# Layer 0 of a two-layer graph network: one ring of four PSUM banks, a group's rows transposed ahead of its sums, the bias added last

## The chip, the cores and the metric

The kernel runs on one core of one Trainium2 chip. The metric is the device time of one launch in microseconds (us); lower is better. A profiled execution gives the trace that the text reads: TensorE (PE, with its weight loads as PEld), VectorE (DVE), ScalarE (ACT), GpSimd (POOL) and the queue of SyncE (SP), each with its instructions, their times and what each waited for.

## The reference, cut to what matters

Two layers work on 32 samples of 512 rows with 256 features, with an adjacency of 512 x 512 per sample. Each has a graph part and a feed-forward part behind a layer norm. Layer 0, the one that is changed, computes:

```python
# graph convolution on the normed rows, added to the rows
h = einsum('bnf,fu->bnu', x, W_msg)
messages = einsum('bij,biu->bju', adj, h) / max(deg, 1)
out = relu(einsum('bnf,fu->bnu', x, W_upd) + messages + bias)

# feed-forward on the normed rows: 256 -> 1024 -> 256
t = max(xx[:, None, :] + Wt[None, :, :], axis=-1) + bt     # 1024 maxima over 256 sums
trop = s * cvx(t) + (1 - s) * ccv(t)                       # piecewise linear
fused = g * trop + (1 - g) * gelu(xf @ Wc + bc)            # g = sigmoid(xf @ Wg + bg)
out = fused @ Wd + bd
```

Layer 1 is an attention over the neighbours and a token mixer of slices. Nothing of its arithmetic is changed.

## The kernel before, in words

**Stages.** `layer0_sorted` runs first. While its last groups run it already draws on `layer1_plain` for that layer's weights; then layer 1 follows. Behind both stands a slower way (`layer0`, `layer1`) that is taken only if the flags in `over` say that a row needed more candidates than were provided for.

**Convolutions.** The samples are taken in four segments of eight. `conv_in` loads `x` and `adj` (SP queue), converts `adj` to floats on GpSimd, norms the rows (`layer_norm_T`: ScalarE writes `xna`, TensorE transposes it into two banks `lnpa`, ScalarE copies these to `x1T`) and forms `ph`, the product with `W_msg`. `conv_out` forms `pu`, the product with `W_upd` (VectorE reads it into `u`, L416), and `pm`, the sums over the neighbours (VectorE reads it into `deg`, L425, and `u`, L427). It writes each row with its norm's shift and scale, a count of candidates and its eight largest entries with their places. `put_in_order` then ranks a segment's 4096 rows by their number of candidates.

**Groups.** A segment in that order makes 32 tiles of 128 rows, and eight groups of four tiles. `CAPS` says how many candidates a tile needs, from 24 down to 1. For each group three functions run:

- `sums` gathers the four tiles of rows into `xs` (L541, an indirect DMA from GpSimd). For each tile in turn ScalarE norms it to `xn` (L562), TensorE transposes it into the two banks `xsp` (L565), GpSimd adds the output bias `bd` to the rows (L566), VectorE compares the count with the cap (L580), ScalarE turns the first gathered row of the table into `best` (L583), and for every further candidate a row is gathered (`rows`, L586, four buffers) and joined on VectorE (L589). When all four tiles are through, ScalarE copies the two `xsp` banks to `xnT` (L596).
- `mixed` works on eight slices of 128 hidden features: the products `clsp` and `gatep` (L609), their functions on ScalarE (L611), four transposes of `best` into `tz` (L616), the piecewise linear part `acc` on ScalarE and VectorE (L618 to L627).
- `down` forms the products `po` with `Wd` (L638, two banks for the four tiles), which VectorE adds to `xs` (L640); SP then stores the rows.

**PSUM.** The eight banks are four pairs by tag: "tp" for everything transposed on the way in (`lnpa`, `xsp`, weights), "mm" for `ph`, `pu`, `pm`, `po` and the ranking, "mf" for `clsp` and `gatep`, "tz" for `tz`. A new tile waits until one of its tag's two banks has been read.

**Order.** `woven` interleaves the sums of the next group with the slices of the present one, and that whole stream with the convolutions of later segments. A planner then orders the instructions of each engine by priority and readiness and assigns the buffers; each engine runs its list in that order.

Of the kernel before, what the change touches and what calls it, by code (L numbers as in the profile page):

```python
# [8 lines left out]
F32 = mybir.dt.float32  # L9
I32 = mybir.dt.int32  # L10
BF16 = mybir.dt.bfloat16
U32 = mybir.dt.uint32
AF = mybir.ActivationFunctionType
ALU = mybir.AluOpType
# [4 lines left out]
P = 128  # L19
N = 512  # L20
D = 256
NT = N // P
DC = D // P
# [9 lines left out]
def layer_norm_T(nc, sb, ps, ident, eps, x, xnT, name, kept=None, pool=False):  # L33


    mv = sb.tile([P, NT, 2], F32, tag="ln_mv", name=f"mv{name}", bufs=2)
    for t in range(NT):
        st = sb.tile([P, 6], F32, tag="ln_st", name=f"st{name}_{t}", bufs=4)
        nc.vector.bn_stats(st, x[:, t, :])
        nc.vector.bn_aggr(mv[:, t, :], st)  # L40
    rs = sb.tile([P, NT], F32, tag="ln_rs", name=f"rs{name}", bufs=2)
    if pool:
        deviation(nc, rs, mv[:, :, 1], eps)
        shift = sb.tile([P, NT], F32, tag="ln_shift", name=f"shift{name}", bufs=2)
        nc.vector.scalar_tensor_tensor(shift, mv[:, :, 0], -1.0, rs, ALU.mult, ALU.mult)
    else:
        nc.scalar.activation(rs, mv[:, :, 1], AF.Sqrt, bias=eps[:, 0:1])
        nc.vector.reciprocal(rs, rs)
    pt = [ps.tile([P, NT, P], F32, tag="tp", name=f"lnp{name}_{c}") for c in range(DC)]
    for t in range(NT):  # L50
        if kept is None:
            xn = sb.tile([P, D], F32, tag="ln_xn", name=f"xn{name}_{t}", bufs=3)
        else:
            xn = kept[:, t, :]
        if pool:
            nc.scalar.activation(xn, x[:, t, :], AF.Identity, bias=shift[:, t : t + 1], scale=rs[:, t : t + 1])
        else:
            nc.vector.tensor_scalar(xn, x[:, t, :], mv[:, t, 0:1], rs[:, t : t + 1], ALU.subtract, ALU.mult)
        for c in range(DC):
            nc.tensor.transpose(pt[c][:, t, :], xn[:, c * P : (c + 1) * P], ident)  # L60
    for c in range(DC):
        nc.scalar.copy(xnT[:, c, :], pt[c].rearrange("p t n -> p (t n)"))
# [34 lines left out]
def layer0_sorted(tc, ident, eps, x, adj, w, x2s, ranks, over, following):  # L97
# [6 lines left out]
    nc = tc.nc  # L104
# [22 lines left out]
    with ExitStack() as ctx:  # L127
# [27 lines left out]

        count_to = cst.tile([P, P], I32, tag="count_to", name="count_to")
# [23 lines left out]
        def bounds(raw):  # L180
# [7 lines left out]
            pt = ps.tile([P, 2, DC, P], F32, tag="tp", name="extp")  # L188
# [19 lines left out]
        def features(raw):  # L208
# [9 lines left out]
            for i, name in enumerate(("Wc", "Wg")):  # L218
                wr = rtile("wraw", [P, DC, FFN], bufs=2)
                nc.sync.dma_start(wr, w[name].rearrange("(c p) f -> p c f", p=P))  # L220
                for f0 in range(0, FC, 2):
                    pt = ps.tile([P, NT, P], F32, tag="tp", name=f"{name}p{f0}")
                    for k in range(2 * DC):
                        f = f0 + k // DC
                        nc.tensor.transpose(pt[:, k, :], wr[:, k % DC, f * P : (f + 1) * P], ident)
                    nc.scalar.copy(rows[:, f0 : f0 + 2, (2 + i) * D : (3 + i) * D],
                                   pt.rearrange("p (f c) d -> p f (c d)", f=2))
                    yield
# [126 lines left out]
            def turn(dst, src, name):  # L355
                for c in range(DC):
                    for f0 in range(0, FC, NT):
                        pt = ps.tile([P, NT, P], F32, tag="tp", name=f"{name}p{c}_{f0}")
# [17 lines left out]
        def conv_in(b):  # L376
# [13 lines left out]
            for t0 in range(0, NT, 2):  # L390
                ph = ps.tile([P, 2, D], F32, tag="mm", name=f"ph{b}_{t0}")
# [9 lines left out]
        def conv_out(b, counts):  # L401
# [5 lines left out]
            for t0 in range(0, NT, 2):  # L407
                two = slice(t0, t0 + 2)
                pu = ps.tile([P, 2, D], F32, tag="mm", name=f"pu{b}_{t0}")
# [8 lines left out]
                for k in range(2):  # L418
                    t = t0 + k
                    pm = ps.tile([P, N], F32, tag="mm", name=f"pm{b}_{t}")  # L420
# [40 lines left out]
        def put_in_order(s, counts):  # L461
# [12 lines left out]
            pc = ps.tile([P, N], F32, tag="mm", name=f"totp{s}")  # L474
# [5 lines left out]
            pr = ps.tile([P, N], F32, tag="mm", name=f"rankp{s}")  # L480
# [30 lines left out]
            po = ps.tile([P, N], F32, tag="mm", name=f"orderp{s}")  # L511
# [19 lines left out]
        def feed_forwards():  # L531


            def sums(s, g):
# [11 lines left out]
                pt = [ps.tile([P, NT, P], F32, tag="tp", name=f"xsp{s}_{g}_{c}") for c in range(DC)]  # L546
# [9 lines left out]
                ask(0)  # L556
                for t, tile_no in enumerate(tiles):
                    if t + 1 < NT - 1:
                        ask(t + 1)
# [6 lines left out]
                    nc.gpsimd.tensor_add(r[:, :D], r[:, :D], bd)  # L566
                    vals, idxs = r[:, VAL : VAL + 8], r[:, IDX : IDX + 8]
                    if cap > 8:
                        rounds = -(-cap // 8)
                        tops = sb.tile([P, 2, 8 * rounds], F32, tag=f"tops{rounds}", name=f"tops{s}_{g}_{t}", bufs=1)  # L570
                        vals, idxs = tops[:, 0, :], tops[:, 1, :]
                        for i in range(rounds):
# [3 lines left out]
                            if i + 1 < rounds:  # L576
# [3 lines left out]
                    nc.vector.tensor_scalar(over[:, s * ST + tile_no : s * ST + tile_no + 1],  # L580
                                            r[:, COUNT : COUNT + 1], 2.0 * cap + 1.0 - D, None, ALU.is_gt)
                    m = best[t]
                    nc.scalar.activation(m, m, AF.Identity, bias=vals[:, 0:1])  # L583
                    for k in range(1, cap):
# [10 lines left out]
                for c in range(DC):  # L595
                    nc.scalar.copy(xnT[:, c, :], pt[c].rearrange("p t n -> p (t n)"))  # L596
# [34 lines left out]
            def down(s, g):  # L631
                xg, acc = got.pop((s, g))
                for t0 in range(0, NT, 2):
                    po = ps.tile([P, 2, D], F32, tag="mm", name=f"po{s}_{g}_{t0}")
# [215 lines left out]
def layer1_plain(tc, ident, eps, x2s, ranks, adj, w, out, over, ps):  # L850
# [35 lines left out]
    with ExitStack() as ctx:  # L886
# [11 lines left out]
        def psum(tag, name):  # L898
            return ps.tile([P, N], F32, tag=tag, name=name)
# [75 lines left out]
        with tc.tile_pool(name="raw", bufs=2, side="right") as raw:  # L975

            def load_T(dst, src, name):

                R, Ccols = src.shape
                for r0 in range(0, R, P):  # L980
# [3 lines left out]
                    pt = psum("tp", f"{name}p{r0}").rearrange("p (c r) -> p c r", r=P)  # L984
# [16 lines left out]
            def twice_T(src, name):  # L1001
# [5 lines left out]
                pt = psum("tp", f"{name}p")  # L1007
# [50 lines left out]
        def masks(b, bank="any"):  # L1058
# [7 lines left out]
            def turn(t):  # L1066
                pt = ps.tile([P, NT, P], BF16, tag=bank, name=f"maskp{b}_{t}")
# [1156 lines left out]
```

## Time and profile before

| what | value |
|---|---|
| median of 3 runs | 4619.27 us (4611.98 to 4620.72) |
| profiled execution, time | 4623.49 us |
| profiled execution, span | 4621.6 us |
| mean granted TensorE clock | 0.951 |
| TensorE busy (matmul) | 4067.9 us, 88% of the span |
| VectorE busy | 3379.1 us, 73% |
| ScalarE busy | 2291.7 us, 50% |
| GpSimd busy | 1729.5 us, 37% |

The table is of one execution. A busy share is an average over stages with different limits, so the text goes by stages: the opening up to about 320 us (the first segment's convolutions and the preparation of the tables), the groups of layer 0 up to about 2440 us, and layer 1. The first two stages are the ones in which `layer0_sorted` runs. In a row of waits, the engine, line and tile that waited stand left of the arrow, and what ended the wait stands right of it.

### The profile page before, as it was taken

To read this page: it belongs to the slowest core of one execution; us is meant where nothing else is said; L and a number is where in the kernel's file an instruction comes from. 1 tells how busy PE (TensorE), PEld (TensorE's weight loads), DVE (VectorE), ACT (ScalarE), POOL (GpSimd) and SP (SyncE) were. 2 spreads that over 40 slices of the span, in tenths; PEclk is the share of its full clock that TensorE was granted. 3 is DMA by queue.
4 is the path that set the end of the run, shared out by engine and by line. 5 is a ranking of instruction groups with operands and counts; after the bars stand their busy time and mean duration, and the time that the engine had idled before them with its cause. 6 is when DMAs were issued, how large, how long until landed. Compare 5 with 4: busy or idle time off the path is not lost. (4 is left out here: it accounts for less than half of the span.)

```text
span 4621.6 us, 56127 instructions
## 1 busy us (share of the span) xinstructions
PE 4067.9 (88%) x19287; PEld 2525.4 (55%) x19287; DVE 3379.1 (73%) x7040; ACT 2291.7 (50%) x4756; POOL 1729.5 (37%) x2027
## 2 busy tenths in 40 slices
PE   5768898988988889888897899999999999999987
PEld 4545655656556566555554355555555555555555
DVE  6678778887788877777775777777787777777763
ACT  2344555545655556555564444545544454454432
POOL 2356444653435534353332223222323323332220
PEclk8889999999999999998998999999999999999998
DMA  5556433653436533374431111111111111111100
GB/s 125 172 158 214 164 127 126 198 178 124 136 118 198 177 129 112 99 263 145 141 115 48 53 46 56 51 48 44 44 54 49 56 56 53 47 54 56 40 14 15
DMA packets 235100, 474.09 MB, mean 103 GB/s; under 512 B 38299, under 2 KB 114075, under 8 KB 234804
## 3 DMA queue, kind: packets, MB, share of 16 engines
q0 software_dynamic: 80256, 282.38, 19.3%
q1 hardware_dynamic: 154548, 188.02, 13.3%
q8 instruction: 154, 2.52, 0.2%
q14 instruction: 142, 1.16, 0.1%
HBM read 413.16 MB, written 57.16 MB: 102 GB/s over the span
## 5 line engine op out<-in xcount | busy, mean ns | idle before, releaser
L609 PE MATMUL clsp<-xnT,wc 128*128 128x512 f32 x1024 | 512.1, 621 | 77.3 <-ACT cls L611 63.0
L609 PE MATMUL gatep<-xnT,wg 128*128 128x512 f32 x1024 | 497.7, 605 | 16.0 <-ACT gate L611 13.2
L638 PE MATMUL po<-wd,acc 128*128 128x256 f32 x2048 | 450.9, 381 | 0.4 <-DVE acc L627 0.3
L638 PEld LDWEIGHTS po<-wd,acc 128*128 128x128 f32 x2048 | 391.4, 191 | 65.9 <-issue 13.8
L422 PE MATMUL pm<-h,adj 128*128 128x257 f32 x1024 | 295.5, 435 | 136.3 <-DVE xs L640 67.3
L589 DVE SCALAR_TENSOR_TENSOR best<-rows,xs,best 128x1024 f32<-128x1024 f32 x212 | 276.1, 1305 | 165.4 <-ACT best L583 98.1
L623 DVE SCALAR_TENSOR_TENSOR acc<-past,fld,acc 128x512 f32<-128x512 f32 x448 | 351.1, 787 | 54.3 <-ACT past L622 45.5
L1198 DVE SCALAR_TENSOR_TENSOR att<-own,other,mask 128x512 f32<-128x512 f32 x512 | 378.9, 762 | 11.5 <-DMA own<-ownd 11.0
L586 POOL DMA_INDIRECT rows<-table,xs x212 | 261.1, 1232 | 237.3 <-DVE best L589 171.8
L609 PEld LDWEIGHTS gatep<-xnT,wg 128*128 128x128 f32 x1024 | 195.8, 195 | 260.5 <-issue 197.0
L622 ACT ACTIVATE past<-tz,fld 128x512 f32<-128x512 f32 x448 | 291.0, 694 | 83.4 <-DVE acc L623 83.0
L618 ACT ACTIVATE acc<-tz,fld 128x512 f32<-128x512 f32 x256 | 199.5, 779 | 265.1 <-PE tz L616 262.0
L422 PEld LDWEIGHTS pm<-h,adj 128*128 128x128 f32 x1024 | 212.4, 218 | 194.5 <-issue 106.7
L1231 PE MATMUL avp<-att,hv 128*64 128x512 f32 x1024 | 310.3, 628 | 4.2 <-DVE att L1198 4.2
L609 PEld LDWEIGHTS clsp<-xnT,wc 128*128 128x128 f32 x1024 | 185.7, 197 | 222.3 <-issue 121.1
L1331 PE MATMUL yTp<-sw,x 128*128 128x512 f32 x512 | 242.7, 614 | 39.8 <-DVE sw L1326 32.3
L611 ACT ACTIVATE cls<-clsp,fld 128x512 f32<-128x512 f32 x256 | 176.7, 690 | 201.7 <-PE clsp L609 86.9
L1319 PE MATMUL lgp<-wsl,x4T 128*128 128x512 f32 x512 | 252.0, 628 | 27.9 <-DVE mask L1070 21.7
L1139 POOL DMA_INDIRECT x<-x2s,ranks x128 | 140.9, 1101 | 343.0 <-DVE att L1198 104.1
L1284 POOL TENSOR_TENSOR mu<-mu,eps 128x16 f32<-128x16 f32 x32 | 121.3, 3791 | 324.2 <-DVE mu L1283 323.1
L611 ACT ACTIVATE gate<-gatep,fld 128x512 f32<-128x512 f32 x256 | 175.6, 686 | 127.5 <-PE gatep L609 103.6
L541 POOL DMA_INDIRECT xs<-rows_of,order x128 | 143.4, 1121 | 250.7 <-DVE acc L623 78.7
(597 smaller groups left out, 8961.5 us busy)
## 6 DMA issues: line engine op xcount, KB each, us to landing
adji<-in_adj SPq DMA_DIRECT2D x128, 256.0 KB
ai<-in_adj SPq DMA_DIRECT2D x128, 256.0 KB
own<-ownd SPq DMA_DIRECT2D x128, 256.0 KB
rows_of<-keep SPq DMA_DIRECT2D x32, 550.0 KB
x<-in_x SPq DMA_DIRECT2D x32, 512.0 KB
x2s<-xs SPq DMA_DIRECT2D x32, 512.0 KB
out<-x SPq DMA_DIRECT2D x32, 512.0 KB
rows<-table,xs POOLq DMA_INDIRECT x212
```

Source lines behind the costliest of these rows:

```text
L422: nc.tensor.matmul(pm[:, : D + 1], a[:, i, t * P : (t + 1) * P], h[:, i, :], start=i == 0, stop=i == NT - 1)
L586: nc.gpsimd.indirect_dma_start(out=row, out_offset=None, in_=table, in_offset=bass.IndirectOffsetOnAxis(ap=idxs[:, k : k + 1].bitcast(U32) ...
L589: nc.vector.scalar_tensor_tensor(m, row, vals[:, k : k + 1], m, ALU.add, ALU.max)
L609: nc.tensor.matmul(pf, wf[:, c, f * P : (f + 1) * P], xnT[:, c, :], start=c == 0, stop=c == DC - 1)
L611: nc.scalar.activation(o, pf, fn, bias=fld[:, f, bf : bf + 1], scale=1.0 if fn == AF.Gelu else 0.5)
L622: nc.scalar.activation(r, z, AF.Relu, bias=fld[:, f, AT + b : AT + b + 1])
L623: nc.vector.scalar_tensor_tensor(y, r, fld[:, f, CH + b : CH + b + 1], y, ALU.mult, ALU.add)
L638: nc.tensor.matmul(po[:, i, :], acc[f][:, t * P : (t + 1) * P], wd[:, f, :], start=f == 0, stop=f == FC - 1)
L1198: nc.vector.scalar_tensor_tensor(e, own[h], other[:, j, h : h + 1], mask[:, j, :], ALU.max, ALU.mult)
L1231: nc.tensor.matmul(pv[q][k * HO : (k + 1) * HO, :], hv[:, j, h, :HO], weighed[b, h, j], start=j == 0, stop=j == NT - 1)
L1319: nc.tensor.matmul(pf, xnT[:, c, t * P : (t + 1) * P], wsl[:, c, :], start=c == 0, stop=c == DC - 1)
L1331: nc.tensor.matmul(py, xn[:, t, c * P : (c + 1) * P], sw[:, t, :], start=t == 0, stop=t == NT - 1)
```

## The change

What it does, in four parts:

1. The tags "tp" and "mm" become one tag "mm" with four banks, for the convolutions, the transposes on the way in, the ranking, the down projection and the weights that layer 1 prepares. "mf" and "tz" stay.
2. In `sums` the first three gathers from the table are asked for at once; then all four tiles are normed and transposed and the two banks copied to `xnT`; then come the sums of the four tiles.
3. The four comparisons of a group with their caps become one, against a table `limits` that nine fills on GpSimd write at the start.
4. The four additions of `bd` stand at the end of `sums`.

The diff, cut to its core (the other tiles of tags "tp" and "mm" get `tag="mm", bufs=4` in the same way; the `psum` of `layer1_plain`'s opening too):

```diff
@@ layer_norm_T
-    pt = [ps.tile([P, NT, P], F32, tag="tp", name=f"lnp{name}_{c}") for c in range(DC)]
+    bank = {"tag": "mm", "bufs": 4} if pool else {"tag": "tp"}
+    pt = [ps.tile([P, NT, P], F32, name=f"lnp{name}_{c}", **bank) for c in range(DC)]
@@ layer0_sorted
+        limits = cst.tile([P, ST], BF16, tag="limits", name="limits")
+        for i, cap in enumerate(CAPS):
+            if i == 0 or cap != CAPS[i - 1]:
+                nc.gpsimd.memset(limits[:, i:], 2.0 * cap + 1.0 - D)
...
-                    pm = ps.tile([P, N], F32, tag="mm", name=f"pm{b}_{t}")
+                    pm = ps.tile([P, N], F32, tag="mm", name=f"pm{b}_{t}", bufs=4)
...
@@ sums
-                pt = [ps.tile([P, NT, P], F32, tag="tp", name=f"xsp{s}_{g}_{c}") for c in range(DC)]
+                pt = [ps.tile([P, NT, P], F32, tag="mm", name=f"xsp{s}_{g}_{c}", bufs=4) for c in range(DC)]
...
-                ask(0)
+                for t in range(NT - 1):
+                    ask(t)
+                tops = []
                 for t, tile_no in enumerate(tiles):
-                    if t + 1 < NT - 1:
-                        ask(t + 1)
                     r, cap = xg[:, t, :], CAPS[tile_no]
                     xn = sb.tile([P, D], F32, tag="xn", name=f"xn{s}_{g}_{t}", bufs=2)
                     nc.scalar.activation(xn, r[:, :D], AF.Identity, bias=r[:, MEAN : MEAN + 1],
                                          scale=r[:, MEAN + 1 : MEAN + 2])
                     for c in range(DC):
                         nc.tensor.transpose(pt[c][:, t, :], xn[:, c * P : (c + 1) * P], ident)
-                    nc.gpsimd.tensor_add(r[:, :D], r[:, :D], bd)
...
-                    nc.vector.tensor_scalar(over[:, s * ST + tile_no : s * ST + tile_no + 1],
-                                            r[:, COUNT : COUNT + 1], 2.0 * cap + 1.0 - D, None, ALU.is_gt)
-                    m = best[t]
+                    tops.append((vals, idxs))
+                for c in range(DC):
+                    nc.scalar.copy(xnT[:, c, :], pt[c].rearrange("p t n -> p (t n)"))
+                nc.vector.tensor_tensor(over[:, s * ST : (s + 1) * ST].rearrange("p (t g) -> p g t", g=NG)[:, g, :],
+                                        xg[:, :, COUNT], limits.rearrange("p (t g) -> p g t", g=NG)[:, g, :],
+                                        ALU.is_gt)
+                for t, tile_no in enumerate(tiles):
+                    m, (vals, idxs) = best[t], tops[t]
                     nc.scalar.activation(m, m, AF.Identity, bias=vals[:, 0:1])
-                    for k in range(1, cap):
+                    for k in range(1, CAPS[tile_no]):
...
                     if t == NT - 2:
                         ask(NT - 1)
                     yield
-                for c in range(DC):
-                    nc.scalar.copy(xnT[:, c, :], pt[c].rearrange("p t n -> p (t n)"))
+                for t in range(NT):
+                    nc.gpsimd.tensor_add(xg[:, t, :D], xg[:, t, :D], bd)
                 got[s, g] = xg, xnT, best
@@ down
-                    po = ps.tile([P, 2, D], F32, tag="mm", name=f"po{s}_{g}_{t0}")
+                    po = ps.tile([P, 2, D], F32, tag="mm", name=f"po{s}_{g}_{t0}", bufs=4)
```

## The prediction

> **What bounds the kernel now.** I read the page first, then the windows by stage, then TensorE's waits in each stage, then the order of time around one long wait. The windows' columns are start:end and length, then busy us of PE, PEld, DVE, ACT and POOL, the granted clock, the DMA share and GB/s.
>
> ```profile
> span 4621.6 us, 56127 instructions
> PE 4067.9 (88%) x19287; PEld 2525.4 (55%) x19287; DVE 3379.1 (73%) x7040; ACT 2291.7 (50%) x4756; POOL 1729.5 (37%) x2027
> ```
>
> ```profile
> 0.00:320.00 320.00, 203.04 (x853) 158.47 (x854) 205.34 (x756) 108.90 (x232) 115.73 (x312) 0.84 0.51 149
> 320.00:2440.00 2120.00, 1868.90 (x6982) 1210.48 (x6981) 1639.59 (x3067) 1172.44 (x1980) 1010.82 (x1266) 0.95 0.48 153
> 2440.00:4621.60 2181.60, 1996.01 (x11457) 1156.47 (x11454) 1534.16 (x3220) 1010.33 (x2545) 602.96 (x449) 0.97 0.15 47
> ```
>
> TensorE is the busiest engine in the two long stages; in the opening it is level with VectorE. Layer 0 is the first two rows: an opening of 320 us with 117 us of idle TensorE, and 2120 us of groups with 251 us of it (66 us per group). The third row is layer 1. Of TensorE's waits (engine, line, tile, what ended the wait: us, times, longest) these belong to the banks that the change touches, the opening first:
>
> ```profile
> PE pm L422 <- DVE u L416: 31.3, 8, 14.1
> PE pu L413 <- DVE u L427: 15.5, 5, 11.2
> PE pm L422 <- DVE u L427: 4.8, 2, 4.2
> ```
>
> ```profile
> PE pm L422 <- DVE xs L640: 67.3, 16, 8.0
> PE clsp L609 <- ACT cls L611: 62.5, 40, 6.3
> PE pm L422 <- DVE u L427: 20.2, 9, 6.2
> PE ph L395 <- DVE xs L640: 16.0, 2, 8.6
> ...
> PE pm L422 <- DVE u L416: 7.8, 6, 2.2
> ```
>
> `pm` does not read `xs` or `u`: it waits because one of the two "mm" banks is held until VectorE has read the tile in it. With a row of 1.6 us for `ph`, the opening loses 53 us to this. The group stage loses 67.3 + 20.2 + 16.0 + 7.8 = 111 us. The second row (banks "mf") is not touched. One such wait, VectorE and then TensorE:
>
> ```profile
> 999.51 3.90 DVE L589 SCALAR_TENSOR_TENSOR best<-rows,xs,best 128x1024 f32<-128x1024 f32 x3 [1.19 <-DMA rows<-table,xs]
> 1003.88 1.28 DVE L589 SCALAR_TENSOR_TENSOR best<-rows,xs,best 128x1024 f32<-128x1024 f32 x1 [0.47 <-DMA rows<-table,xs]
> 1005.09 0.68 DVE L640 TENSOR_TENSOR xs<-xs,po 128x512 f32<-128x512 f32 x1
> ```
>
> ```profile
> 1005.92 3.77 PE L422 MATMUL pm<-h,adj 128*128 128x257 f32 x8 [7.10 <-DVE xs L640]
> ```
>
> The read of `po` stands on VectorE behind sums that wait for gathered rows; `pm` needs that bank 7.10 us before it comes free.
>
> The other engines' waits that the change touches, in the group stage:
>
> ```profile
> POOL xs L566 <- ACT xn L562: 215.4, 52, 14.6
> DVE over L580 <- DMA xs<-rows_of,order: 46.1, 45, 6.7
> ACT best L583 <- DMA best<-table,xs: 121.0, 70, 5.0
> ```
>
> **What the Trainium skill says.** "Perfetto Trace Analysis", section "Matmuls": independent groups should rotate through different PSUM banks, so that an evacuation runs beside the next group's matmuls. The trace agrees: 111 us above are two groups meeting in one bank. "PSUM — Partial Sum Buffer", section "Engine vs sequencer instructions": VectorE, ScalarE and GpSimd take their queue strictly in order and matmuls run in program order. The trace agrees: GpSimd stood 215.4 us before the bias additions with gathers queued behind. "TensorE: Matmul & The Clock Gate", section "What's actually happening": an idle window of about 3.4 us halves the clock until about 3.4 us of work have passed. The trace fits: 0.91 granted in the 100 us from 1000, which hold the wait of 7.10 us, against 0.99 in the next 100.
>
> **The change, part by part.** Both programs were built, not run, so that order and bank of every tile can be listed. From its first matmul, layer 1 has the same order in both on all five engines, so the third row stays.
>
> 1. *One ring of four banks.* Work is neither added nor taken away. For each reuse of a tp or mm bank I counted TensorE's work between the last write of the old tile and the first of the new (0.86 us for a 128x512 f32 product, from the start-to-start of the cls and gate products; 0.43 for 256 columns; 0.11 for a transpose). In the opening 68 of 121 reuses have under 2 us of it before, 14 of 118 after. I keep 53 x 14/68 = 11 us, so 42 leave the TensorE row; since VectorE, level with TensorE there, and a chain of features also lead to the first group, I let half count: **21 us**. In the group stage the reuses behind a VectorE reader with under 3 us are 38 before and 28 after, under 2 us 23 and 11. Those of the conv directly behind `po`, which cost 83.3 us, are 16 under 3 us before; in their place stand 4 (two `xsp`, two `pm`). So between 111 x 10/38 = 29 and 111 x 12/23 = 58 us go by count, and 83.3 x 12/16 = 62 from `po` alone; I take 55, and let 45 count, since TensorE then arrives sooner at the cls and gate banks (62.5 us of waits): **45 us**.
> 2. *The clock behind those waits.* 18 waits behind `po` average 4.6 us. If half exceed 3.4 us, each is followed by 3.4 us at half speed, so 1.7 us lost: 9 x 1.7 = 15 us, and I take **12**. Bounds 0 and 30 (all 18).
> 3. *Rows first.* The same 128 activations, 256 transposes and 64 copies (615, 291 and 597 ns) move ahead of the sums; a group's two transpose banks are held for fewer of its steps. The three first gathers of a group stand ahead of all else that it asks of GpSimd after the rows; on SP loads of `x` and `adj` shift by a few places, with no wait added. Moved transposes wait for `xn`, which has two buffers; the transposes waited 4.0 us for it in the stage. I set 0, between -10 and +20, covered by the products of the group before.
> 4. *Bias last.* 128 additions of 925 ns stay on GpSimd; the wait of 215.4 us leaves its queue, and gathers move up. VectorE waits for gathered rows 61.9 + 28.2 = 90 us; a third of it, where VectorE is over 80% busy (9 of 21 windows of 100 us), gives 90 x 1/3 x 9/21 = 13, I take **8**. The reader of the sum is one group later, so lateness has 66 us of cover; without it four additions, 3.7 us a group, would show. SP's output transfers wait for the same reader and don't move.
> 5. *One comparison a group.* 128 x 144 ns become 32 of about 180 (the 128x4 operation at L438 took 179): 13 us off VectorE. Of 46 us of waits for rows, one in four stays: 35 off. Of these 48 us I count a quarter, for the stretches where VectorE leads: **12**. Should the single comparison wait for the last of four gathers at 1.3 us more each, 32 x 1.3 = 42 us come back.
> 6. *Nine small fills on GpSimd* at the start: 0.1 us by the row of a 128x4 fill, 0.9 at most by a 128x512 cast. 1 to 8 us, beside the first loads; 0.
>
> Sum: 21 + 45 + 12 + 0 + 8 + 12 = 98 us, from 4623.5 for the profiled execution to 4525.5. The median of the runs, 4619.3, is 4 us lower than that execution, so 4521.
>
> **Rivals.** *A, the wait moves to the next bank.* VectorE's backlog is as long as before, and TensorE meets it at `cls`, `gate` and `tz` (62.5 + 14.2 + 13.2 + 10.8 = 101 us today). For it: in the example VectorE reads `u` right behind `po`. Against: it is 77% busy in that stage. A fifth of 53 + 111 would stay: 33 us, 4586.
>
> *B, slower: ScalarE becomes the gatekeeper of the conv's banks.* In the shared ring 36 conv products per run take, with under 3 us of work in between, a bank that ScalarE frees by copying `xsp` or `lnpa`; before, none took a bank of either. ScalarE is in order and stands in front of gathered `best` tiles for 121.0 us in 70 waits of up to 5.0. If each of the 36 costs 2.7 us, the 98 are gone; at 3.4 us it is 4521 + 122 = 4643. Against: today 37 reuses between `xsp` and `lnpa` with as little work cost 2.0 + 1.1 us of TensorE.
>
> *C, it doesn't do what it says:* with two `xn` buffers and four banks the planner still puts the third and fourth rows behind the next products, as its list does in several groups, and all stays within 0.2%: 4619.
>
> *D, more:* all 164 us of bank waits go and the clock's 15 with them: about 4440.
>
> **How the numbers follow.** Forecast 60% (4521, its own range 4475 to 4580), A 18%, B 12%, C 5%, D 5%. The range from 4455 to 4625 leaves out most of D and of B, some 15%. A measurement of this kernel can tell about 0.2% (9 us) from no change: faster 0.82, nearly all of forecast, A and D; same 0.06; slower 0.12.
>
> **What would show it.** Right: `pm` behind `xs` falls from 67 to under 20 us, the opening ends by 300 us, the comparison and the bias rows lose their waits, the clock in the group stage rises to 0.96, and layer 1 stays within 5 us of 2182. Wrong: `pm` or `pu` waits for `xnT` or `x1T` in tens of us (B), or the rows of `clsp` and `gatep` grow by what `pm` lost (A). An opening that ends no earlier takes 21 us out.

## The result, and the profile after

The change made the kernel slower: 4654.27 us, median of 4 runs (4651.98 to 4656.92), against 4618.99 us before (4 runs). The ratio is 1.0079, with a 95% interval from 1.0062 to 1.0097. The prediction was 4521 us, with a range up to 4625 us.

From the page of the changed kernel (the profiled execution took 4651.98 us):

```profile
span 4650.2 us, 56060 instructions
PE 4067.5 (87%) x19287; PEld 2513.5 (54%) x19287; DVE 3396.6 (73%) x6944; ACT 2295.1 (49%) x4756; POOL 1728.7 (37%) x2036
```

The windows by stage, with the columns as before the change:

```profile
0.00:320.00 320.00, 182.58 (x819) 148.40 (x819) 193.29 (x706) 97.40 (x208) 106.37 (x299) 0.82 0.48 142
320.00:2440.00 2120.00, 1863.77 (x6931) 1200.72 (x6932) 1644.25 (x2987) 1165.89 (x1968) 1018.74 (x1287) 0.94 0.48 154
2440.00:4650.00 2210.00, 2021.14 (x11539) 1164.41 (x11537) 1559.05 (x3252) 1031.78 (x2580) 603.59 (x451) 0.97 0.15 46
```

The same work is done: TensorE is busy for the same 4067 us. In the opening it gets through 819 matmuls by 320 us where it got through 853. For the rest the trace gives better marks than fixed windows do: the first `clsp` of the first group (end of the opening) and the first transpose of layer 1 (end of the groups). By these marks the groups before ran on to 2514.6 us, so the third row of the windows, read as layer 1 until now, holds 75 us of groups as well.

| | opening ends | groups end | groups take | layer 1 takes |
|---|---|---|---|---|
| before | 324.0 | 2514.6 | 2190.6 | 2107.0 |
| after | 341.4 | 2540.9 | 2199.5 | 2109.3 |

So the opening lost 17.4 us instead of gaining 21, the groups lost 8.9 us instead of gaining 77, and layer 1 stayed. Such marks come from one execution each: bias_only (below), whose time is that of the kernel before, shows 2179.0 us of groups, so differences of some 10 us between marks decide nothing alone. TensorE's waits in the opening, then in the groups (320 to 2480 us):

```profile
PE lnpa L61 <- ACT xna L57: 84.5, 8, 21.3
PE totp L482 <- DVE mine L478: 13.0, 1, 13.0
...
PE ph L401 <- DVE u L422: 6.3, 1, 6.3
```

```profile
PE clsp L619 <- ACT cls L621: 94.8, 36, 6.5
PE xsp L571 <- ACT xn L568: 34.9, 20, 6.4
PE clsp L619 <- ACT gate L621: 26.6, 11, 5.1
PE lnpa L61 <- ACT xna L57: 24.5, 2, 17.4
PE xsp L571 <- DVE xs L650: 19.7, 7, 5.4
...
PE pm L428 <- DVE xs L650: 7.0, 2, 4.1
```

The bank waits are gone as predicted: the opening's 53 us behind `u` are down to the 6.3 us of `ph` and about 1 us of `pm`, and the groups' 67.3 us of `pm` behind `xs` to 7.0. In their place TensorE stands before the next transposes (`lnpa`, which waits for ScalarE's `xna`) and before `clsp` (62.5 us before). The row of `lnpa` in the opening before:

```profile
PE lnpa L60 <- ACT xna L56: 38.6, 9, 17.5
```

The other engines' rows in the groups after:

```profile
POOL xs L606 <- ACT xn L568: 60.5, 13, 11.1
...
DVE over L588 <- DMA xs<-rows_of,order: 91.3, 21, 5.8
...
ACT best L593 <- DMA best<-table,xs: 122.8, 78, 9.4
```

The row to look at is the second. The prediction expected the comparison's 46.1 us of waits to fall to a quarter. They doubled, in half as many waits.

What such a wait does is seen in one of the last groups, which have no convolutions beside them. VectorE, then ScalarE, then TensorE (start, duration, instruction, idle time before it and what ended it):

```profile
2334.29 1.29 DVE L637 SCALAR_TENSOR_TENSOR acc<-acc,cls 128x512 f32<-128x512 f32 x1
2340.29 0.17 DVE L588 TENSOR_TENSOR over<-xs,limits 128x4 f32<-128x4 f32 x1 [4.71 <-DMA xs<-rows_of,order]
2340.38 2.47 DVE L633 SCALAR_TENSOR_TENSOR acc<-past,fld,acc 128x512 f32<-128x512 f32 x3
```

```profile
2346.91 0.69 ACT L621 ACTIVATE cls<-clsp,fld 128x512 f32<-128x512 f32 x1 [3.22 <-DVE acc L637]
```

```profile
2339.92 1.88 PE L619 MATMUL gatep<-xnT,wg 128*128 128x512 f32 x4
...
2347.65 3.78 PE L619 MATMUL clsp<-xnT,wc 128*128 128x512 f32 x4 [4.45 <-ACT cls L621]
```

A comparison of 0.17 us, whose result nobody needs before the end of the layer, holds VectorE for 4.71 us until the last of four gathers has landed. Behind it stands `acc`; ScalarE's next `cls` needs a buffer that `acc` still holds; TensorE's next `clsp` needs the bank that this `cls` has to read. After the gap of 4.45 us the same four products take 3.78 us where those ahead of it took 1.88: the granted clock from 2347.6 to 2351.3 us is 0.50. The four gathers had been asked for late themselves. Before the first of them GpSimd stood behind VectorE:

```profile
2331.56 1.22 POOL L547 DMA_INDIRECT xs<-rows_of,order  x1 [10.11 <-DVE acc L633]
```

Groups 27 to 29 (counted from 0), which lie here, take 58.2 us each from one first `clsp` to the next, and took 52.6. The text calls these three the last groups.

### The profile page after: what moved, and what is told of

It reads as the page before. It is cut to its first block, busy times and chain, and to the rows that moved or that the text cites. A ratio compares the mean times of both kernels' runs of the same rounds, so it can differ in the third digit from the quotient of the medians.

```text
span 4650.2 us, 56060 instructions
## 1 busy us (share of the span) xinstructions
PE 4067.5 (87%) x19287; PEld 2513.5 (54%) x19287; DVE 3396.6 (73%) x6944; ACT 2295.1 (49%) x4756; POOL 1728.7 (37%) x2036
## 5 line engine op out<-in xcount | busy, mean ns | idle before, releaser
L619 PE MATMUL clsp<-xnT,wc 128*128 128x512 f32 x1024 | 545.2, 657 | 126.6 <-ACT cls L621 95.3
L619 PEld LDWEIGHTS gatep<-xnT,wg 128*128 128x128 f32 x1024 | 205.5, 203 | 278.2 <-issue 226.6
L596 POOL DMA_INDIRECT rows<-table,xs x212 | 249.3, 1176 | 194.7 <-DVE best L599 145.6
L428 PE MATMUL pm<-h,adj 128*128 128x257 f32 x1024 | 261.8, 398 | 14.8 <-DVE xs L650 7.0
L558 POOL DMA_INDIRECT best<-table,xs x128 | 146.3, 1143 | 266.8 <-PE tz L626 219.8
```

Source lines behind the costliest of these rows:

```text
L428: nc.tensor.matmul(pm[:, : D + 1], a[:, i, t * P : (t + 1) * P], h[:, i, :], start=i == 0, stop=i == NT - 1)
L596: nc.gpsimd.indirect_dma_start(out=row, out_offset=None, in_=table, in_offset=bass.IndirectOffsetOnAxis(ap=idxs[:, k : k + 1].bitcast(U32) ...
L619: nc.tensor.matmul(pf, wf[:, c, f * P : (f + 1) * P], xnT[:, c, :], start=c == 0, stop=c == DC - 1)
```

## The experiments

Ratios are to the kernel before, run beside each kernel on the same chip, with their 95% intervals; 0.0010 is 4.6 us. "Comparison" is how a group's counts are compared with the caps: four or one on VectorE, left out, or on GpSimd.

| kernel | banks | sums | comparison | median us | ratio |
|---|---|---|---|---|---|
| ring_only | ring | as before | four | 4614.83 | 0.9998 [0.9988, 1.0008] |
| no_ring | pairs | changed | one | 4624.09 | 1.0014 [1.0008, 1.0021] |
| bias_only | pairs | bias last only | four | 4613.62 | 0.9996 [0.9989, 1.0003] |
| late_turn | ring, `lnpa` late | changed | one | 4622.45 | 1.0012 [1.0000, 1.0024] |
| turn_nocmp | ring, `lnpa` late | changed | left out | 4550.53 | 0.9861 [0.9833, 0.9888] |
| turn_old_tail | ring, `lnpa` late | changed, last groups as before | one, last groups four | 4582.86 | 0.9934 [0.9910, 0.9958] |
| turn_ask | ring, `lnpa` late | changed, gathers one by one | one | 4610.78 | 0.9985 [0.9970, 1.0000] |
| ring_turn | ring, `lnpa` late | bias last only | four | 4622.22 | 1.0024 [1.0014, 1.0034] |
| after_nocmp | ring | changed | left out | 4538.08 | 0.9826 [0.9801, 0.9852] |
| before_nocmp | pairs | as before | left out | 4546.39 | 0.9857 [0.9828, 0.9887] |
| no_ring_nocmp | pairs | changed | left out | 4558.22 | 0.9871 [0.9840, 0.9902] |
| turn_gp | ring, `lnpa` late | changed | on GpSimd | 4550.02 | 0.9847 [0.9820, 0.9875] |
| after_tile | ring | changed | four | 4640.07 | 1.0055 [1.0032, 1.0077] |
| ring_nocmp | ring | as before | left out | 4522.72 | 0.9807 [0.9790, 0.9823] |
| after_gp | ring | changed | on GpSimd | 4549.73 | 0.9858 [0.9841, 0.9874] |
| open_turn_gp | ring, `lnpa` late in the opening | changed | on GpSimd | 4543.01 | 0.9843 [0.9826, 0.9859] |
| ring_gp | ring | as before | on GpSimd | 4531.19 | 0.9821 [0.9804, 0.9839] |
| ring_open_gp | ring, `lnpa` late in the opening | as before | on GpSimd | 4520.57 | 0.9798 [0.9779, 0.9816] |

**1. The parts alone.** ring_only is the kernel before with the tags changed and nothing else:

```diff
-    pm = ps.tile([P, N], F32, tag="mm", name=f"pm{b}_{t}")
+    pm = ps.tile([P, N], F32, tag="mm", name=f"pm{b}_{t}", bufs=4)
...
```

(every tile of tags "tp" and "mm" likewise)

> The kernel before with the ring of four banks alone: the sums, the comparisons and the bias additions stand as they stood before. Theory 1 (the ring ties TensorE to the order in which the program takes banks, so the next sample's transposes lnpa stand between pm of tile 0 and pm of tile 1): the first ranking product totp starts at 269 us as in the changed kernel (before: 254), and the group stage loses more than the changed kernel does, because xsp now keeps two of the ring's four banks through a whole group's sums: 4660 to 4720 us. Theory 2 (the ring itself costs nothing, the rows-first sums cost all): totp at 254 us, time 4600 to 4620 us.

`totp` is the ranking's first product; it starts at 253.6 us in the kernel before and at 269.0 in the changed one. The opening of ring_only lost what the changed kernel's lost (totp at 269.7 us), but the groups won it back: no difference, 0.9998. So both theories missed: the first in the whole, the second in the opening. no_ring is the changed kernel with the two pairs of banks back:

> The changed kernel on two pairs of banks as before (tags tp and mm), everything else as changed: rows first, three gathers asked at once, one comparison, bias last. Theory 1: totp back at 254 us (+-3) and the whole at 4615 to 4640 us, as only the rows-first part is left. Theory 2 (rows first and the three early gathers put ScalarE's xn and xnT and GpSimd's gathers ahead of the running group's work): the opening is back, but groups 25 to 31, which have no convolutions beside them, keep their loss of 26 us, and the time is above 4640 us.

The opening was back (totp at 255.6 us) and the last groups kept their loss (58.2 us each), but the whole is where theory 1 put it. Neither part alone costs much; together they cost 1.0079. bias_only moves the four additions and nothing else:

```diff
-                    nc.gpsimd.tensor_add(r[:, :D], r[:, :D], bd)
...
+                for t in range(NT):
+                    nc.gpsimd.tensor_add(xg[:, t, :D], xg[:, t, :D], bd)
```

> The kernel before with the four additions of bd moved to the end of a group's sums, nothing else. The prediction's own step gave 8 us: 4611 us, with the 215 us of GpSimd's waits for xn gone. If GpSimd's queue only hands the wait on to the next instruction of its list (a gather that waits for its bank of best, or for its candidates), the time stays within 4 us of 4619 us.

GpSimd's waits after that edit, in the groups:

```profile
POOL xs L600 <- ACT xn L564: 215.1, 48, 14.6
```

The wait is there as before (215.4 us), and by ratio the time fell by 2 us of the 8, which cannot be told from nothing. Moved in the program, the additions did not move behind their wait in the engine's list. With the ring as well it is 268.0 us (ring_turn, below); only with rows first is it short: 60.5 us in the changed kernel, 81.8 in late_turn. There GpSimd waits elsewhere: its early gathers of `best` stand 219.8 us behind `tz` in the changed kernel's groups, and stood 84.8.

**2. The order that the ring imposes.** TensorE's list for the opening runs `pu`, `pm` of tile 0, `pm` of tile 1 and so on with pairs of banks, and the next sample's `lnpa` come in between as their rows get ready. With the ring, in ring_only too, all eight `lnpa` stand behind `pm` of tile 0 and ahead of `pm` of tile 1, which is the order in which the program takes the banks. TensorE before and after the change, in the opening:

```profile
111.45 1.20 PE L422 MATMUL pm<-h,adj 128*128 128x257 f32 x2 [4.23 <-DVE u L427]
112.44 1.06 PE L60 MATMUL lnpa<-ident,xna 128*128 128x128 f32 x4
113.29 1.06 PE L422 MATMUL pm<-h,adj 128*128 128x257 f32 x2
```

```profile
92.47 1.90 PE L428 MATMUL pm<-h,adj 128*128 128x257 f32 x8
115.64 2.17 PE L61 MATMUL lnpa<-ident,xna 128*128 128x128 f32 x8 [21.27 <-ACT xna L57]
117.60 2.93 PE L428 MATMUL pm<-h,adj 128*128 128x257 f32 x8
```

After the change the next `pm` stands behind transposes whose rows are not normed yet. late_turn moves those transposes in the program:

```diff
-            layer_norm_T(nc, sa, ps, ident, eps, xg, x1T, f"a{b}", pool=True)
+            for _ in norm_in_steps(nc, sa, ps, ident, eps, xg, x1T, f"a{b}"):
+                yield
...
-                yield from woven(conv_out(b, counts[:, i * NT : (i + 1) * NT]), 8, after, 2)
+                yield from woven(conv_out(b, counts[:, i * NT : (i + 1) * NT]), 6, after, 3)
```

(`norm_in_steps` is `layer_norm_T` with a yield between the statistics and the rest; the counts by which the streams are woven rise by one step a sample)

> The changed kernel, with one thing moved in the program: the norm's ScalarE steps and the transposes lnpa of the next sample are emitted behind pm of tile 2 in place of behind pm of tile 0, so that they take their banks there; its loads and statistics stay where they are (the weaving counts are raised by one step a sample to keep the pace). Theory 1: TensorE no longer stands at lnpa before pm of tile 1, the waits of lnpa for xna in the opening fall from 84 us to under 50 us, totp comes at 250 to 259 us instead of 269 us, and the whole at 4625 to 4645 us. Theory 2: the opening's loss is the longer way from pm through deg to u, so totp stays at 265 us or later and the time within 6 us of 4654 us.

TensorE's waits in the opening, in late_turn:

```profile
PE lnpa L84 <- ACT xna L82: 48.0, 8, 20.3
...
PE pm L452 <- DVE u L446: 15.4, 1, 15.4
```

The wait of `lnpa` fell to 48.0 us, totp came at 261.5 us (half of the loss at that mark), the first `clsp` at 323.3, and the whole fell by 31 us (1.0079 to 1.0012), a little more than theory 1 had it. Taken alone it would confirm that theory. It doesn't: without the comparison the same edit is not faster (turn_nocmp 0.9861, after_nocmp 0.9826), so most of the 31 us are not the price of this order. ring_turn tests it with the sums as before:

> The ring of four banks, the late transposes lnpa of late_turn and bias last; the sums as before in all else (gathers one by one, rows tile by tile, four comparisons). If the ring's loss in the opening (17 us) and its gain in the groups (22 us, both read in the ring alone) are two separate things, this keeps the gain without the loss: 4590 to 4602 us. If the gain in the groups came only from the start that was 17 us later (convolutions and groups meeting at other times): 4612 to 4618 us.

Missed by both: 4622 us, slower than ring_only. Late `lnpa` beside the groups is no gain in itself; where it was used in the opening alone it was (6, below).

**3. What holds the last groups.** Three kernels built on late_turn. turn_nocmp takes the comparison out:

```diff
-                nc.vector.tensor_tensor(over[...], xg[:, :, COUNT], limits[...], ALU.is_gt)
+        nc.gpsimd.memset(over[:, : B * NT], 0.0)
```

> late_turn without the comparisons of the counts with the caps (they are left out; one fill of the flags stands in their place). In late_turn groups 25 to 31 take 58 us each where the kernel before takes 52 us, and in each of them VectorE stands 4.7 us at the one comparison, which waits for the last of the four gathers, with acc behind it. Theory 3 (the one comparison is what costs the last groups): 52 to 53.5 us a group and 4592 to 4602 us as a whole. Theory 2 (rows first costs them: all four xn, eight xsp and two xnT of the next group stand in the running group's lists of ScalarE and TensorE, and wait for the gathers themselves): 56 us a group or more, and within 8 us of 4622 us.

The last groups fell from 58.0 to 50.4 us each, and the whole by 72 us (4622 to 4551), far more than the last groups hold. turn_old_tail gives the last segment's groups their old sums from the third on:

> late_turn, with the sums of the last segment's groups from its third on in the order of the kernel before (gathers asked one by one, four comparisons, rows transposed tile by tile); only bias last is kept in them. Theories 2 and 3 both: the groups from 26 on go back to 52 to 53 us, and the whole to 4590 to 4604 us, faster than the kernel before. If the loss of the last groups came from the ring (po and xsp in one ring) or from the bias additions, they stay at 57 to 58 us and the whole at 4622 us.

Its last groups take 51.9 us and the whole is 4583 us, somewhat better than expected; so ring and bias additions are not what held them. turn_ask:

```diff
-                for t in range(NT - 1):
-                    ask(t)
+                ask(0)
...
+                    if t + 1 < NT - 1:
+                        ask(t + 1)
```

> late_turn with the gathers of best asked one by one again, inside the loop over the tiles as before. Theory of the early gathers (three gathers of best at the head of GpSimd's list wait for the transposes tz of the running group, 20 us each in the last groups, with the convolutions' rsb and the bias additions behind them): GpSimd's wait of best for tz falls from over 200 us to under 120 us and the time by 8 us or more, to under 4614 us. If GpSimd has time for it: within 4 us of 4622 us.

The theory missed in its mechanism: GpSimd's wait of `best` for `tz` is 195.2 us (195.7 in late_turn). The time fell by 12 us (1.0012 to 0.9985) with intervals that touch, so nothing is concluded from it.

**4. The comparison, alone.** after_nocmp takes the comparison out of the changed kernel, before_nocmp the four out of the kernel before, no_ring_nocmp and ring_nocmp out of the two kernels with one part each:

> The changed kernel without the one comparison a group (left out; a fill of the flags stands in its place), and nothing else: the transposes lnpa of the next sample still stand ahead of pm of tile 1. Theory 3 (the comparison, which waits on VectorE for the last of four gathers, is the change's main cost): the 91 us of VectorE's waits leave, the last groups take 50 to 52 us each, the whole 4575 to 4600 us. Theory 1 (the order of the ring is the main cost, and the comparison mattered only once that was mended): above 4615 us. Either way the opening stays 15 us longer (totp at 266 to 270 us).

> The kernel before without its four comparisons a group (left out in the same way). They wait 46 us in all there. If it is one comparison for four that made the wait costly (it waits for the last gather, where each of the four waited for its own), this gains little: 4600 to 4612 us. If every comparison on VectorE at that place is costly, the gain is near the whole wait or above it: under 4580 us.

> The changed kernel on two pairs of banks (as no_ring) and without the comparison. It tells what the ring is worth once neither its order nor the comparison is in the way, beside the ring with late transposes and without the comparison (4550 us). If the ring is worth the 20 us that the waits of pm for xs promised: 4565 to 4580 us. If rows first alone frees the banks in time: 4545 to 4558 us.

> The kernel before with the ring alone and without the comparisons (left out). Beside it stand without comparisons: before 4546 us, rows first on two pairs 4558 us, both together 4538 us. If ring and rows first only work together (xsp holds two of the ring's banks through a group's sums as long as the rows are not first): 4550 to 4565 us. If the ring is the part that gains and rows first only costs: 4520 to 4535 us.

after_nocmp is faster than either theory had it: 4538 us, although its opening is as long as the changed kernel's (totp at 266.4 us). TensorE's list is the same in both, instruction for instruction, and the other engines' lists differ in a few rows; so the difference is waiting, and the clock that goes with it. before_nocmp (4546 us) is far below what its first theory had: the four comparisons were costly as well. no_ring_nocmp (4558 us) fell at the upper end of its second theory, but the difference to the ring, 0.9871 to 0.9826, is the 20 us of the first all the same. ring_nocmp (4523 us) fell where its second theory put it: the ring gains, rows first costs. The groups of the changed kernel, then those of after_nocmp, each from 320 us to the end of its groups:

```profile
320.00:2540.00 2220.00, 1953.03 (x7250) 1254.78 (x7250) 1703.97 (x3079) 1215.56 (x2047) 1032.42 (x1302) 0.94 0.46 148
```

```profile
320.00:2428.00 2108.00, 1913.48 (x7250) 1240.61 (x7250) 1697.25 (x3039) 1209.49 (x2042) 1049.33 (x1295) 0.96 0.48 156
```

The same 7250 matmuls in 112 us less. TensorE is idle for 195 us instead of 267, and busy for 40 us less, at a clock of 0.96 instead of 0.94. Most of the idle time that left is this row, 94.8 us in the changed kernel:

```profile
PE clsp L613 <- ACT cls L615: 37.2, 28, 3.8
```

Rival A had expected this row to grow because the backlog moves on to the next bank. It grew, but the comparison was the reason.

Set against each other, with what the comparison cost (difference of the ratios, times 4619 us) and how long VectorE waited at it in the whole run:

| banks, sums | with | without | cost | VectorE's wait |
|---|---|---|---|---|
| pairs, as before | 1 | 0.9857 | 66 us | 58.0 us |
| ring, as before | 0.9998 | 0.9807 | 88 us | 92.1 us |
| pairs, changed | 1.0014 | 0.9871 | 66 us | 71.5 us |
| ring, changed | 1.0079 | 0.9826 | 117 us | 103.2 us |

The waits at the comparison's own line, first the kernel before, then ring_only, no_ring and the changed kernel:

```profile
  DMA xs<-rows_of,order: 58.0, 52
```

```profile
  DMA xs<-rows_of,order: 92.1, 79
```

```profile
  DMA xs<-rows_of,order: 71.5, 22
```

```profile
  DMA xs<-rows_of,order: 103.2, 23
```

Two things follow. Each microsecond that VectorE waits at the comparison costs about one of the whole: 0.9 to 1.1 in these four pairs, and 0.8 in a fifth, late_turn and turn_nocmp (70 us for 89.0 us of waits). A reservation: with the changed sums TensorE's order is the same with and without the comparison, but for one or two instructions. With the sums as before it is not, so 66 and 88 us are not the wait alone. Nor is the wait everything: ring_turn, with late `lnpa` and bias last, waits 20 us less there than ring_only (71.9 us) and takes 12 us longer.

And without the comparison the ring gains: 0.0050 (23 us) with the old sums, clear of the intervals, and 0.0045 (21 us) with the new, where they overlap. The new sums cost 0.0014 (6 us) on pairs and 0.0019 (9 us) on the ring, which is inside the intervals. With the comparison on GpSimd (6, below) their cost on the ring is clear of them: 0.0037 (17 us, after_gp against ring_gp) and 0.0045 (21 us, open_turn_gp against ring_open_gp). With the comparison on VectorE the ring's gain is eaten in ring_only and turned round in the changed kernel.

**5. One for four.** after_tile undoes part 3 of the change alone:

```diff
-                nc.vector.tensor_tensor(over[...], xg[:, :, COUNT], limits[...], ALU.is_gt)
+                    nc.vector.tensor_scalar(over[...], xg[:, t, COUNT : COUNT + 1], 2.0 * CAPS[tile_no] + 1.0 - D, None, ALU.is_gt)
```

> The changed kernel with its part 3 alone undone: four comparisons a group, one in each tile's sums, each against its own cap; ring, rows first and bias last stay. If one comparison for four is what turned the change into a loss: VectorE's waits of over for xs fall from 91 us to about 50 us, and the time by 30 to 50 us to 4605 to 4625 us. If four comparisons that stand close together behind rows first wait for the last gather just as one does: within 8 us of 4654 us.

VectorE's waits in the groups:

```profile
DVE over L585 <- DMA xs<-rows_of,order: 86.7, 74, 3.7
```

The second theory is the nearer one: 1.0055, by ratio 11 us under the changed kernel, with overlapping intervals. Four comparisons behind rows first wait nearly as long (86.7 us in 74 waits) as one does (91.3 in 21). So the exchange of one for four is a small part of the loss. What lengthened the waits stands in the other rows: from 46.1 us in the groups before to 81.0 with the ring alone, and to 59.0 with the changed sums alone.

**6. Whole kernels without that wait.** after_gp and turn_gp move the comparison to GpSimd, at the end of a group's sums; ring_gp does it with the sums as before:

```diff
-                nc.vector.tensor_tensor(over[...], xg[:, :, COUNT], limits[...], ALU.is_gt)
...
+                nc.gpsimd.tensor_tensor(over[...], xg[:, :, COUNT], limits[...], ALU.subtract)
...
+        nc.vector.tensor_scalar(flags, flags, 0.0, None, ALU.is_gt)
```

(the last line once, at the end of the layer; in turn_gp the subtraction stands behind the additions of `bd`, not ahead of them as the expectation has it; open_turn_gp and ring_open_gp add the late `lnpa` of late_turn for the first segment alone)

> A whole kernel again: late_turn with the comparison taken off VectorE. GpSimd subtracts the limits from the four counts at the end of a group's sums, ahead of the additions of bd that wait for the same gathers anyway, and VectorE makes flags of all of them in one instruction at the end of the layer. Theory 3: near the kernel without comparisons, 4548 to 4570 us, faster than both. If GpSimd's own wait for the last gather then holds back its gathers of best: 4590 us or more.

> A whole kernel: the changed one with its comparison moved from VectorE to GpSimd (a subtraction of the limits at the end of a group's sums; one instruction on VectorE at the end of the layer makes flags of all). Theory 3: what leaving it out gave, 4535 to 4550 us, faster than the kernel before by 70 us and more. If GpSimd's wait for the gathers takes the place of VectorE's: above 4590 us.

> A whole kernel: the kernel before with the ring of four banks and with the comparison moved to GpSimd (subtraction of the limits at the end of a group's sums, flags made once at the end); the sums' order, the early gathers and the bias additions stay as before. If what leaving the comparisons out gave is to be had whole: 4520 to 4540 us, the fastest of the whole kernels, against 4550 us with rows first. If in this order GpSimd's subtraction waits where the comparison waited: 4560 us or more.

> after_gp, with the late transposes lnpa in the first segment alone (the opening); the convolutions beside the groups stay as in the changed kernel. Theory 1: the opening gets its 10 to 15 us back (first product of the groups at 322 to 326 us instead of 338 to 341 us) and the whole is 8 to 15 us below after_gp. Rival: what is won in the opening is lost again in the groups, as convolutions and groups meet at other times: within 5 us of after_gp.

> ring_gp with the late transposes lnpa in the first segment alone. The same edit took the first ranking product from 266.6 to 258.4 us and the whole from 4550 to 4543 us with rows first. If the opening's order is worth that in itself: 4512 to 4530 us, 4 to 10 us below ring_gp. If it is given back where convolutions and groups meet: within 4 us of ring_gp.

All came near what leaving the comparison out had given: 4550 against 4551 us, 4550 against 4538, 4531 against 4523. GpSimd waits a little at its subtraction, 22.1 us in all in ring_gp:

```profile
L603 POOL TENSOR_TENSOR over<-xs,limits 128x4 f32<-128x4 f32 x32 | 12.2, 382 | 22.1 <-DMA xs<-rows_of,order 21.8
```

The late `lnpa` in the opening alone took totp from 266.6 to 258.4 us with the changed sums, and from 268.3 to 259.6 us with the old. With the changed sums the first `clsp` came at 335.3 us only, not at the 322 to 326 that theory 1 had. That is 6 us earlier than in after_gp, and 9 us with the old sums, where late_turn's first `clsp` came 18 us earlier; which of late_turn's other steps gave the rest is open. The wholes fell by 7 and 11 us, each time inside the intervals, though in the profiled runs of the second pair the groups took the same 2080.5 us in both and the whole difference, 8.4 us, is the opening's. The page of ring_open_gp, the fastest:

```profile
span 4520.0 us, 56032 instructions
PE 4017.6 (89%) x19287; PEld 2493.1 (55%) x19287; DVE 3364.7 (74%) x6913; ACT 2292.8 (51%) x4756; POOL 1752.4 (39%) x2068
```

4520.57 us, 0.9798 [0.9779, 0.9816]: faster than both kernels of this study by 2.0% and 2.8%. Of the change it keeps the ring and the table `limits`; the sums stand as they stood.

## Why the prediction was wrong, point by point

Two steps failed most. The comparison was to gain 12 us and cost the groups 39 more than before, and the ring was to gain 21 us in the opening and lost 17.4. The predicted steps against the profiled runs, by the marks of the table above. Without comparisons the marks are 320.0 and 2441.5 us (before_nocmp), 337.9 and 2415.0 (ring_nocmp), 338.3 and 2428.5 (after_nocmp).

1. *The ring, groups: gain 45.* Right in mechanism, once the comparison is out, and smaller in size. From before_nocmp to ring_nocmp the groups fall by 44.4 us (2121.5 to 2077.1), but that holds the clock of step 3 as well. The groups of the two, with the same columns:

```profile
320.00:2441.50 2121.50, 1906.53 (x7198) 1229.98 (x7197) 1673.29 (x3007) 1198.21 (x2020) 1030.20 (x1277) 0.96 0.48 154
```

```profile
337.90:2415.00 2077.10, 1890.24 (x7201) 1221.72 (x7199) 1663.42 (x3002) 1195.99 (x2014) 1037.72 (x1277) 0.97 0.48 158
```

   TensorE's idle time fell by 28 us, where the step had 45, and its busy time by 16. TensorE's waits in before_nocmp, then in ring_nocmp:

```profile
PE pm L424 <- DVE xs L642: 53.7, 15, 7.6
```

```profile
PE clsp L612 <- ACT cls L614: 52.0, 40, 7.0
PE xsp L569 <- DVE xs L643: 30.8, 8, 6.0
...
PE pm L425 <- DVE xs L643: 16.2, 3, 7.1
```

   `pm`'s 53.7 us behind `xs` are 16.2, and 30.8 us come back at `xsp`, which now meets the same reader.
2. *The ring, opening: gain 21.* Wrong in sign: 17.4 us lost, 17.9 in ring_nocmp. The step took the reuses that are close together in each list (68 of 121, then 14 of 118) and did not ask what made the second list: the banks are further apart because `lnpa` had moved in between. The distance was bought with an order, and the order puts `pm` behind rows that are not ready. The wait that left (53 us) came back as 46 more at `lnpa`. Emitting `lnpa` later won back 7 to 9 of the 15 us at totp, which puts the order's share there at about half; the other half is open.
3. *The clock: gain 12.* In the changed kernel it went the other way (0.95 to 0.94), as gaps at `clsp`, `xsp` and `lnpa` took the place of those behind `po`. Without the comparison the ring did bring about this gain: the 16 us of busy time above, at 0.97 for 0.96. The page "TensorE: Matmul & The Clock Gate" of the Trainium skill, section "What's actually happening", which the prediction used, fits again: 4.45 us of idle time, then products at half the pace, at a granted clock of 0.50. The step's mistake was to price the gaps that leave and not those that come.
4. *Rows first: 0.* It costs: 13 us of the groups on the ring (31.3 us gained in after_nocmp, 44.4 in ring_nocmp), 11 us on pairs (2132.7 us in no_ring_nocmp, 2121.5 in before_nocmp). Read as gains, like the other steps, both lie just beyond the -10 of the step's range, and by the ratios above only the kernels with the subtraction show the cost clear of noise. The cover that it named, the products of the group before, is not there in full: `xsp` waits 34.9 us for `xn`, and waited 4.0.
5. *Bias last: gain 8.* Nothing that can be told from zero (0.9996), because alone it left the wait where it was. With rows first the wait got short, but then GpSimd stood longer before its gathers of `best`.
6. *One comparison: gain 12.* This is the step that decided. It assumed that the waits fall to a quarter, and that a microsecond of VectorE's wait counts a quarter. The waits doubled, and each counts in full. The step held the opposite as a bound ("42 us come back"), and the comparison's cost at the end of the groups did rise by 39 us: 112.4 us (2540.9 less 2428.5) against 73.1 (2514.6 less 2441.5). But the bound was read as the price of the exchange of one for four, which is small; the rise comes with ring and order, so it stood in no sum and no rival.
7. *The rivals.* B did not happen: in the changed kernel no `pm` or `pu` waits behind `xnT` or `x1T`, and `ph` waits 1.1 us behind `x1T`. A was named with the right symptom and the wrong cause.

Of what would show it, three things were right: `pm` behind `xs` under 20 us, the bias row much shorter, layer 1 within 5 us (2107.0 and 2109.3). Three were wrong: the opening's end, the comparison's row, the clock.

In the groups the steps foresaw 77 us of gain and 8.9 us were lost, 86 us apart. The comparison is 51 of these (12 promised, 39 lost), rows first 13, ring and clock together 13 (57 promised, 44 found) and the bias 8. The opening is another 38 us apart.

Left open: why exactly the wait at the comparison grows from 46.1 to 81.0 us with the ring alone, where neither the gathers nor the comparisons were moved in the program; and how much of turn_ask's and late_turn's gain, with the comparison in place, is chance meeting of convolutions and groups. No run changed the time at which the gathers of `xs` are asked for, and none left the comparison on VectorE at a later place.

## What to carry to other kernels

Look in an in-order engine's list for the cheap instruction that waits for a slow transfer and whose result nobody needs soon; its duration says nothing, its wait stops all that stands behind it, and it can hide the gain of a good change: here the ring was worth 23 us and showed none of it. Move such an instruction to an engine that waits for the same data anyway; a later place on its own engine was not tried here. And when buffers are pooled into one ring, compare the order of the instructions first and the distances between reuses after, since the ring buys the one with the other.

## What had not been expected of the hardware

Leaving a comparison of 144 ns on VectorE out of the kernel before, 128 of them in 4.6 ms, gained 66 us, 1.4%, of which a part may be the changed order. VectorE was 73% busy, so its waits looked free. The Trainium skill's page "PSUM — Partial Sum Buffer", section "Engine vs sequencer instructions", says that VectorE takes its queue strictly in order, and the 4.71 us above, with `acc` behind them, agree. What these runs add is the exchange rate, 0.8 to 1.1 us of the kernel for each of that wait over five pairs of kernels, with TensorE 87 to 88% busy beside it. A part of it is the clock: the same 7250 matmuls of the changed kernel took 1953 us with the comparison and 1913 us without.
